# Layer 0 of a four-layer graph network: the one-hot edge types with edges along the columns, turned by TensorE before, loaded from memory after

## The chip, the cores and the metric

The kernel runs on one core of a Trainium2 chip. The metric is the device time of one execution in microseconds (us), the median of several runs. A core has five engines that run side by side, each through its own queue of instructions in order: TensorE (PE in the profile, its weight loads PEld), VectorE (DVE), ScalarE (ACT), GpSimd (POOL) and SyncE (SP), which here does nothing but start DMAs. An instruction may wait on semaphores that other engines or DMAs raise; while it waits, everything behind it in the same queue waits too. Sixteen DMA engines move data between memory (DRAM) and the on-chip buffer of 128 partitions (SBUF).

## What is computed

Four graph layers on 3125 nodes of 256 features and 50000 edges sorted by destination, each followed by a residual and a layer norm. The change touches layer 0 alone:

```python
e = edge_emb[edge_type]                       # 16 types
att_in = concat([x[src], x[dst], e, task])    # per edge, 4*256
edge_delta = tanh(gelu(att_in @ att_W1 + att_b1) @ att_W2 + att_b2)
edge_weight = 1.0 + edge_scale * edge_delta
messages = ((x[src] + e) @ msg_W + msg_b) * (1 + 0.5*tanh(gamma)) + beta
agg = segment_sum(messages * edge_weight, dst) / max(segment_sum(edge_weight, dst), 1)
# then an update MLP on [x, agg] and a layer norm
```

The kernel splits `att_in @ att_W1` into four products: the parts of the source and destination nodes are worked out once per node, the part of the type once per type (`ec`), and each edge adds three rows.

## The kernel before

**Tiling.** Edges are laid out by `bucket` into 416 slot tiles (`TT`) of 128 edges, one edge per partition; every slot tile belongs to one tile of 128 destination nodes (`tnode`). `s_src`, `s_dl` (place of the destination in its node tile) and `s_ty` (type) hold one column per slot tile. `segments` works out tables for the later layers, in four chunks of up to 128 slot tiles, with the slot tile on the partition and the edge along the columns; it writes `seg` and `rows` to DRAM.

**Layer 0's edge loop** (end of `layer0`) takes G = 4 slot tiles at a time, 104 groups, in a software pipeline: one turn of the loop issues `gathered` of group i, `attended` of group i-1 and `summed` of group i-2.

- `gathered(t0)`: four indirect DMAs on POOL (L509) fetch each edge's source row into `gb` (5 buffers; 640 floats a row: x and three bf16 thirds of its product, together the fp32 product). DVE builds the one-hot `oh[:, 0]` of destination places (L928), the one-hot of types (L931) in the first 16 columns of `gb`, and copies the latter three times side by side in bf16 into `oh[:, 1]` (L934, 48 of 128 columns; the rest was set to zero once, L918). TensorE transposes both (L939, eight 128x128 bf16 transposes into one PSUM tile `ohp`), and ACT copies the result to SBUF (L943, 128x1024), which gives `oht`: places, and types, with edges along the columns. Once every two groups SP stores the pair's places and turned places to `oh_d` and `oht_d` (L946), which layers 1 and 2 read.
- `attended`: per slot tile three products with `idb` add the source thirds (L956, two slot tiles at once), three products of the turned places with `xb` add the destination thirds (L961), and one product of the turned types with `ec` adds the type's part (L964; `ec` holds three bf16 thirds of the type product in rows 0 to 47). ACT applies GELU (L965), DVE multiplies by `att_W2` and sums (L967).
- `summed`: ACT takes tanh (L972), scales (L973) and weighs the places by the result (L976, `ohw`), TensorE sums the 128 edges of each slot tile by node (L979 into `pa`, three PSUM buffers), and DVE adds that to the accumulator (L981).

**What sets the order.** The Tile framework orders each engine's queue when the kernel is built, from dependencies and its own estimates, and inserts the semaphore waits; a buffer is written again only when all readers of the tile that held it are done. In the order built here PE runs, per turn: the transposes of group i+2, `attended` of group i+1 (L956, L961, L964 for two slot tiles, then again for two), the sums of group i (L979). DVE runs: two adds (L981) of group i-1 with the builds of types between them (L931, L934), the build of places (L928), two products L967, the first add of the next group, two more products L967, and so on. The fourth sum of a group needs the PSUM buffer that the first add of the same group frees, as `pa` has three.

Of the kernel before, what the change touches and what calls it, by code (L numbers as in the profile page):

```python
# [9 lines left out]
F32 = mybir.dt.float32  # L10
BF = mybir.dt.bfloat16
# [7 lines left out]
P = 128  # L19
# [14 lines left out]
class Net:  # L34
# [178 lines left out]
    def bucket(self, src, dst, type16, type8, weight, relations):  # L213
# [22 lines left out]
        self.seg = self.dram.tile([TT, 5, P], F32, name="seg")  # L236

        self.rows = self.dram.tile([NS, 2, S], F32, name="rows")
        self.astart, self.aend, self.anew = (c.tile([1, TT], F32, name=n) for n in ("astart", "aend", "anew"))
        self.tnode = c.tile([1, TT], I32, name="tnode")  # L240

        with tc.tile_pool(name="bk", bufs=1, side="right") as b:
# [40 lines left out]
            with tc.tile_pool(name="bkw", bufs=1, side="right") as w, tc.tile_pool(name="bkp", bufs=1, space=PSUM) as ps:  # L283
# [71 lines left out]
                nc.vector.tensor_single_scalar(bat, bat, D, op=ALU.mult)  # L355
                nc.scalar.dma_start(self.b_at, bat)

                self.segments(w, bd, nxt, prv, bdf, sel, kd)

    def segments(self, w, bd, nxt, prv, bdf, sel, kd):  # L360

        tc, nc, TT = self.tc, self.nc, self.TT
        C = bd.shape[1]
        flag = w.tile([P, 2, C, P], F32, name="flag")
        nc.vector.tensor_tensor(flag[:, 0], prv, bd, op=ALU.not_equal)
        nc.vector.tensor_tensor(flag[:, 1], nxt, bd, op=ALU.not_equal)
        zero = w.tile([P, P], F32, name="zero")
        nc.vector.memset(zero, 0.0)
        with tc.tile_pool(name="sgp", bufs=1, space=PSUM) as ps, tc.tile_pool(name="sg", bufs=2, side="right") as v:
            rows = ps.tile([1, 3, 512], F32, name="rows")  # L370
            for m0 in range(0, TT, P):
                M = min(P, TT - m0)
# [12 lines left out]
                nc.vector.tensor_scalar(low[:M], low[:M], float(P), None, op0=ALU.mult)  # L385
                sg = v.tile([P, 5, P], F32, name="sg")
                dl = v.tile([P, P], F32, name="dl")
                nc.vector.tensor_scalar(dl[:M], pk[:M, 0, :], low[:M], None, op0=ALU.subtract)
                ins = v.tile([P, P], F32, name="ins")
                nc.vector.tensor_scalar(ins[:M], dl[:M], 0.0, None, op0=ALU.is_ge)  # L390
                nc.vector.scalar_tensor_tensor(ins[:M], dl[:M], float(P), ins[:M], op0=ALU.is_lt, op1=ALU.mult)
                nc.vector.tensor_scalar(sg[:M, 0], ins[:M], -1.0, -NEG, op0=ALU.add, op1=ALU.mult)
                for n in (1, 2):
                    nc.vector.scalar_tensor_tensor(sg[:M, n], pk[:M, n, :], NEG, ins[:M],
                                                   op0=ALU.mult, op1=ALU.mult)
                nc.vector.tensor_tensor_scan(sg[:M, 3], zero[:M], sg[:M, 1], 0.0, op0=ALU.add, op1=ALU.min)
# [357 lines left out]
    def layer0(self, task, edge_emb, msg_W, msg_b, att_W1, att_b1, att_W2, att_b2, edge_scale,  # L754
# [9 lines left out]
        with ExitStack() as layer:  # L764
# [21 lines left out]
            ub2 = vec(up_b2, D, "ub2")  # L786
            lng = vec(ln_g, D, "lng")
            lnb = vec(ln_b, D, "lnb")
            ec = wp.tile([P, D], BF, name="ec")
            nc.vector.memset(ec, 0.0)  # L790
            one = wp.tile([P, 1], F32, name="one1")
            nc.vector.memset(one, 1.0)
            me = wp.tile([ET, D], F32, name="me")
# [2 lines left out]
            with tc.tile_pool(name="n0", bufs=2) as w, tc.tile_pool(name="m0", bufs=1) as wm, \  # L796
# [21 lines left out]
                E3 = 3 * ET  # L818
# [61 lines left out]
                nc.vector.tensor_scalar(fst[:, 2:3], self.pidx[:E3], float(2 * ET), None, op0=ALU.is_ge)  # L880
                nc.vector.tensor_add(fst[:, 1:2], fst[:, 0:1], fst[:, 2:3])
                nc.vector.tensor_scalar(fst[:, 1:2], fst[:, 1:2], -1.0, 1.0, op0=ALU.mult, op1=ALU.add)
                nc.vector.tensor_scalar(ecs, part[:, 0, :], fst[:, 0:1], None, op0=ALU.mult)
                for n, o in ((1, ecs), (2, ec[:E3])):
                    nc.vector.scalar_tensor_tensor(o, part[:, n, :], fst[:, n:n + 1], ecs,
# [25 lines left out]
            with tc.tile_pool(name="e0g", bufs=5) as gp, tc.tile_pool(name="e0", bufs=3) as w, \  # L911
# [1 line left out]

                places = [hp.tile([P, 2, 2, G, P], BF, name="places%d" % n) for n in range(2)]
                for n, oh in enumerate(places):
                    (nc.vector if n % 2 else nc.gpsimd).memset(oh[:, 1], 0.0)  # L918
                ohts = [None]

                def gathered(t0):
                    gb = gp.tile([P, G, ET + XA], F32, name="gb")
                    for j in range(G):
                        self.gather(gb[:, j, ET:], table, self.s_src, t0 + j)
                    g = t0 // G % 2
                    both = places[t0 // (2 * G) % len(places)]
                    oh = both[:, :, g]
                    nc.vector.tensor_tensor(  # L928
                        oh[:, 0], self.iota[:, None, :].to_broadcast([P, G, P]),
                        self.s_dl[:, t0:t0 + G][:, :, None].to_broadcast([P, G, P]), op=ALU.is_equal)  # L930
                    nc.vector.tensor_tensor(  # L931
                        gb[:, :, 0:ET], self.iota[:, None, :ET].to_broadcast([P, G, ET]),
                        self.s_ty[:, t0:t0 + G][:, :, None].to_broadcast([P, G, ET]), op=ALU.is_equal)
                    nc.vector.tensor_copy(oh[:, 1, :, 0:3 * ET].rearrange("p j (n e) -> p j n e", n=3),  # L934
                                          gb[:, :, None, 0:ET].to_broadcast([P, G, 3, ET]))
                    pt = ps.tile([P, 2, G, P], BF, name="ohp")
                    for n in range(2):
                        for j in range(G):
                            nc.tensor.transpose(pt[:, n, j, :], oh[:, n, j, :], self.idb)  # L939
                    if not g:  # L940
                        ohts[0] = hp.tile([P, 2, 2, G, P], BF, name="oht", bufs=2)
                    oht = ohts[0][:, :, g]
                    nc.scalar.copy(oht, pt)  # L943
                    if g:
                        for to, of in ((self.oh_d, both), (self.oht_d, ohts[0])):
                            nc.sync.dma_start(to[t0 // (2 * G)], of[:, 0].rearrange("p g j v -> p (g j v)"))  # L946
                    return t0, gb, oh, oht

                def attended(t0, gb, oh, oht):
                    hg = w.tile([P, G, D], F32, name="hg", bufs=2)  # L950
                    dl = w.tile([P, G], F32, name="dl")
                    for j0 in range(0, G, 2):
# [4 lines left out]
                        for j in (j0, j0 + 1):  # L957
                            q = pre[:, j - j0, :]
                            node = self.node_of(nc.tensor, t0 + j)
                            for n in range(3):  # L960
                                last = nc.tensor.matmul(q, oht[:, 0, j, :], xbr[:, ds(node * (3 * D) + n * D, D)],  # L961
                                                        start=False, stop=False)
                            self.used(nc.tensor, last)
                            nc.tensor.matmul(q, oht[:, 1, j, :], ec, start=False, stop=j > j0)  # L964
                        nc.scalar.activation(hg[:, j0:j0 + 2, :], pre, AF.Gelu)  # L965
                        for j in (j0, j0 + 1):
                            nc.vector.scalar_tensor_tensor(hg[:, j, :], hg[:, j, :], 1.0, aw2, op0=ALU.mult,  # L967
# [3 lines left out]
                def summed(t0, gb, oh, dl):  # L971
# [1 line left out]
                    nc.scalar.activation(dl, dl, AF.Identity, bias=one, scale=esc)  # L973
                    ohw = w.tile([P, G, P], F32, name="ohw", bufs=2)
                    for j in range(G):
                        nc.scalar.activation(ohw[:, j, :], oh[:, 0, j, :], AF.Copy, scale=dl[:, j:j + 1])  # L976
                    for j in range(G):
                        pa = ps.tile([P, SW], F32, name="pa", bufs=3)
                        nc.tensor.matmul(pa, ohw[:, j, :], gb[:, j, 0:ET + D], start=True, stop=True)  # L979
# [656 lines left out]
```

## Time and profile before

| | us |
|---|---|
| median of 3 runs (3344.36 to 3361.28) | 3351.46 |
| the profiled execution, whole | 3366.77 |
| its span, first to last instruction | 3365.0 |
| setup, sorting into slot tiles, node products of layer 0 | 0 to 215 |
| layer 0's edge loop | 215 to 800 |
| layer 0's node update, node products of layer 1 | 800 to 1170 |
| layer 1's edges, and its node update | 1170 to 1800 to 1970 |
| layer 2's edges, and its node update | 1970 to 2670 to 2830 |
| layer 3's edges and the output | 2830 to 3365 |

The stage bounds are read from the first and last starts of each stage's instructions. In the table of the span in 40 slices one slice is 84.1 us, so layer 0's edge loop is a little over half of the third slice up to the middle of the tenth. A group line of the profile gives line, engine, operation, output<-inputs, shape and count, then busy time and the mean of one, then the idle time before it and what ended most of that. A timeline line gives start, duration, engine, line, operation, count, and in brackets the idle time just before and what ended it.

### The profile page before, as it was taken

The numbers are of one execution on the slowest core, as the hardware profiler recorded it, in microseconds if no ns is written. First come the engines' busy times: TensorE is split into PE (matmuls) and PEld (weight loads), VectorE is DVE, ScalarE is ACT, GpSimd is POOL, SyncE is SP. The second block draws the span as 40 slices with busy tenths as digits, with TensorE's granted clock in tenths as the row PEclk, the third lists the DMA queues.
The fourth block names the chain that finished last, engine by engine and source line by source line (L and its number), as shares of the span: only waits on it lengthen the run. The fifth ranks groups of instructions, "written<-read, shape, count | busy, mean of one in ns | idle before, by whom it ended". The sixth has DMA issues, their size and how long they took to land. (4 is left out here: it accounts for less than half of the span.)

```text
span 3365.0 us, 50575 instructions
## 1 busy us (share of the span) xinstructions
PE 2690.9 (80%) x12679; PEld 1750.5 (52%) x12679; DVE 2267.3 (67%) x6030; ACT 1460.9 (43%) x4405; POOL 1832.7 (54%) x1850
## 2 busy tenths in 40 slices
PE   2779999999979767777775847888888886888885
PEld 1357777775546345555553525666666664333333
DVE  2546676667655479888886437888888873555555
ACT  1427777774456334545543215656656553000001
POOL 3037777771044166666661556766766202777773
PEclk9889999999989878888887968888888886656566
DMA  7249998894067877777774367877877235333333
GB/s 164 74 134 296 298 289 290 288 287 141 32 248 285 313 224 241 231 235 233 231 232 132 123 209 200 227 226 223 228 223 225 78 125 221 106 106 105 105 106 92
DMA packets 240632, 658.40 MB, mean 196 GB/s; under 512 B 47976, under 2 KB 87028, under 8 KB 234029
## 3 DMA queue, kind: packets, MB, share of 16 engines
q0 software_dynamic: 132400, 484.37, 46.9%
q1 hardware_dynamic: 104278, 167.53, 15.2%
q10 hardware_dynamic: 3676, 3.23, 0.5%
q8 instruction: 122, 2.00, 0.2%
q14 instruction: 156, 1.28, 0.1%
HBM read 513.06 MB, written 151.58 MB: 198 GB/s over the span
## 5 line engine op out<-in xcount | busy, mean ns | idle before, releaser
L509 POOL DMA_INDIRECT gb<-table,s_src x832 | 859.1, 1033 | 371.6 <-issue 201.2
L706 PE MATMUL pr<-r,oh 128*128 128x260 f32 x2496 | 735.8, 441 | 82.2 <-DVE acc L711 32.6
L706 PEld LDWEIGHTS pr<-r,oh 128*128 128x128 f32 x2496 | 503.2, 217 | 219.5 <-issue 37.2
L1509 POOL DMA_INDIRECT ring<-table,b_rel x391 | 369.7, 946 | 317.9 <-DVE oh L1519 199.1
L701 ACT ACTIVATE r<-gb,ex 128x64 f32<-128x64 f32 x2080 | 522.3, 335 | 0.0
L509 POOL DMA_INDIRECT gb<-table,s_rel x416 | 404.4, 972 | 205.8 <-issue 110.0
L711 DVE TENSOR_TENSOR acc<-acc,pr 128x260 f32 (+1 forms) x832 | 457.9, 550 | 73.0 <-PE pr L706 59.4
L1538 PE MATMUL pa<-ring,oh 128*128 x832 | 420.5, 617 | 92.3 <-DMA ring<-table,b_rel 44.6
L1538 PEld LDWEIGHTS pa<-ring,oh 128*128 128x128 f32 x832 | 190.7, 278 | 322.4 <-DVE oh L1519 210.8
L1545 DVE TENSOR_TENSOR x<-x,pa 128x256 f32 x416 | 175.2, 421 | 227.8 <-PE pa L1538 225.6
L1237 PE MATMUL pqe<-q_all,oht 128*128 x1248 | 207.1, 304 | 94.6 <-DVE pd L1242 78.7
L693 ACT CAST oh<-ohb 128x512 f32<-128x512 bf16 x208 | 128.3, 618 | 314.2 <-PE pr L706 284.3
L589 ACT ACTIVATE r<-mv,eps 128x4 f32<-128x4 f32 (+2 forms) x31 | 9.1, 295 | 527.8 <-DVE mv L575 524.4
L697 DVE TENSOR_TENSOR r<-gb,ex 128x512 f32<-128x512 f32 (+1 forms) x208 | 225.7, 1086 | 13.3 <-ACT ex L666 9.0
L979 PE MATMUL pa<-gb,ohw 128*128 128x272 f32 x832 | 223.4, 402 | 4.5 <-DVE acc L981 2.9
L1237 PEld LDWEIGHTS <-oht 128*128 128x128 bf16 x1248 | 130.6, 106 | 128.4 <-issue 87.6
L961 PE MATMUL pre<-xb,oht 128*128 x1248 | 193.7, 273 | 0.0
L981 DVE TENSOR_TENSOR acc<-acc,pa 128x272 f32 x416 | 179.7, 432 | 5.1 <-PE pa L979 2.8
L928 DVE TENSOR_TENSOR places<-iota,s_dl 128x512 bf16<-128x512 f32 x104 | 71.9, 691 | 160.8 <-ACT ohw L976 160.8
L956 PE MATMUL pre<-gb,idb 128*128 128x512 bf16 x624 | 169.3, 380 | 5.3 <-DMA gb<-table,s_src 5.3
L967 DVE SCALAR_TENSOR_TENSOR hg<-hg,aw 128x256 f32<-128x256 f32 x416 | 159.3, 420 | 16.4 <-ACT hg L965 16.4
L979 PEld LDWEIGHTS pa<-gb,ohw 128*128 128x128 f32 x832 | 141.2, 190 | 54.6 <-issue 34.0
(383 smaller groups left out, 4302.0 us busy)
## 6 DMA issues: line engine op xcount, KB each, us to landing
ohb<-oh_d SPq DMA_DIRECT2D x104, 256.0 KB
oht<-oht_d SPq DMA_DIRECT2D x104, 256.0 KB
table<-row SPq DMA_DIRECT2D x25, 1024.0 KB
gb<-table,s_src POOLq DMA_INDIRECT x832, 4.5
oh_d<-places SPq DMA_DIRECT2D x52, 256.0 KB
oht_d<-oht SPq DMA_DIRECT2D x52, 256.0 KB
sgm<-seg SPq DMA_DIRECT2D x26, 320.0 KB
gb<-table,s_rel POOLq DMA_INDIRECT x416, 4.7
```

What stands on the lines that cost most here:

```text
L509: self.nc.gpsimd.indirect_dma_start(out=out, out_offset=None, in_=table, in_offset=bass.IndirectOffsetOnAxis(ap=idx[:, t:t + 1], axis=0))
L697: nc.vector.tensor_mul(r[:, :, :nd, :hw], v[:, :, :nd, :], ex[:, :nd, s0:s0 + G].rearrange("p h t -> p t h")[:, :, :, None].to_broadcast([ ...
L701: nc.scalar.activation(r[:, j, h, :hw], v[:, j, h, :], AF.Copy, scale=ex[:, h, s0 + j:s0 + j + 1])
L706: nc.tensor.matmul(pr[:, n, :HB * F], oh[:, j, :], r[:, j, n * HB:(n + 1) * HB, :].rearrange("p h f -> p (h f)"), start=True, stop=True)
L711: self.used(nc.vector, nc.vector.tensor_add(a, a, pr[:, :, :HB * F]))
L961: last = nc.tensor.matmul(q, oht[:, 0, j, :], xbr[:, ds(node * (3 * D) + n * D, D)], start=False, stop=False)
L979: nc.tensor.matmul(pa, ohw[:, j, :], gb[:, j, 0:ET + D], start=True, stop=True)
L981: self.used(nc.vector, nc.vector.tensor_add(a, a, pa))
L1237: last = nc.tensor.matmul(pq[:, j, :], oht[:, j, :], q_all[:, ds(node * (3 * D) + n * D, D)], start=n == 0, stop=n == 2)
L1509: st = nc.gpsimd.indirect_dma_start(out=ring[:, at:at + D], out_offset=None, in_=table, in_offset=bass.IndirectOffsetOnAxis(ap=b_rel[:, b: ...
L1538: last = nc.tensor.matmul(pa, oh[:, j, :], ring[:, ds(at, D)], start=True, stop=True)
L1545: self.used(nc.vector, nc.vector.tensor_add(a, a, pa))
```

## The change

The types with edges along the columns no longer come from `gathered`.

- `segments` multiplies the selection of each chunk with the types too (four more fp32 products into the PSUM tile `pk`, behind the reading of its last column), ACT copies the result to bf16, and SP stores it in a new DRAM tensor `ty_d`: one row of 128 types per slot tile.
- For every pair of groups (8 slot tiles) `spread` loads the 1024 types, 2 KB, into all 128 partitions: one DMA of 128 rows of 2 KB that all come from the same 2 KB of DRAM, 256 KB written. The tile `types` has three buffers. The load for pair k+1 is asked for at the start of pair k.
- `attended` begins with a DVE comparison in place (128x512 bf16): each partition's own type number, `own` (0 to 15 three times, -1 from partition 48 on), against the loaded types. This is the one-hot that the product with `ec` takes.
- Four of the eight transposes, the DVE copy (L934) and half of ACT's copy (L943) go, as does the clearing of the old tiles on DVE and POOL.
- `places` and `oht` are now tiles of a pair of groups, two buffers each, taken anew for every pair, where `places` were two fixed tiles before.

```diff
-                places = [hp.tile([P, 2, 2, G, P], BF, name="places%d" % n) for n in range(2)]
-                for n, oh in enumerate(places):
-                    (nc.vector if n % 2 else nc.gpsimd).memset(oh[:, 1], 0.0)
-                ohts = [None]
+                both, types_of = [None], [None]
+
+                def spread(t0):
+                    types_of[0] = t = hp.tile([P, 2, G, P], BF, name="types", bufs=3)
+                    nc.sync.dma_start(t.rearrange("p g j e -> p (g j e)"), bass.AP(
+                        tensor=self.ty_d.tensor, offset=self.ty_d.offset + t0 * P, ap=[[0, P], [1, 2 * G * P]]))
+
+                spread(0)
...
                     g = t0 // G % 2
-                    both = places[t0 // (2 * G) % len(places)]
-                    oh = both[:, :, g]
+                    if not g:
+                        both[0] = [hp.tile([p, 2, G, P], BF, name=n, bufs=2) for p, n in (
+                            (P, "places"), (P, "oht"))] + [types_of[0]]
+                        if t0 + 2 * G < TT:
+                            spread(t0 + 2 * G)
+                    oh, oht, ty = (b[:, g] for b in both[0])
...
-                    nc.vector.tensor_copy(oh[:, 1, :, 0:3 * ET].rearrange("p j (n e) -> p j n e", n=3),
-                                          gb[:, :, None, 0:ET].to_broadcast([P, G, 3, ET]))
-                    pt = ps.tile([P, 2, G, P], BF, name="ohp")
-                    for n in range(2):
-                        for j in range(G):
-                            nc.tensor.transpose(pt[:, n, j, :], oh[:, n, j, :], self.idb)
-                    if not g:
-                        ohts[0] = hp.tile([P, 2, 2, G, P], BF, name="oht", bufs=2)
-                    oht = ohts[0][:, :, g]
+                    pt = ps.tile([P, G, P], BF, name="ohp")
+                    for j in range(G):
+                        nc.tensor.transpose(pt[:, j, :], oh[:, j, :], self.idb)
                     nc.scalar.copy(oht, pt)
...
+                def attended(t0, gb, oh, oht, ty):
+                    nc.vector.tensor_scalar(ty, ty, own, None, op0=ALU.is_equal)
...
-                            nc.tensor.matmul(q, oht[:, 1, j, :], ec, start=False, stop=j > j0)
+                            nc.tensor.matmul(q, ty[:, j, :], ec, start=False, stop=j > j0)
...
+                for k in range(C):
+                    nc.tensor.matmul(pk[:M, 3, :], sel[:, k, m0:m0 + M], f16[:, k, :], start=k == 0, stop=k == C - 1)
+                ty = v.tile([P, P], BF, name="ty")
+                nc.scalar.copy(ty[:M], pk[:M, 3, :])
+                nc.sync.dma_start(self.ty_d[m0:m0 + M], ty[:M])
```

More of the change, by code (lines that the diff above doesn't have):

```diff
@@ L238, in bucket @@
         self.rows = self.dram.tile([NS, 2, S], F32, name="rows")
+        self.ty_d = self.dram.tile([TT, P], BF, name="ty_d")
         self.astart, self.aend, self.anew = (c.tile([1, TT], F32, name=n) for n in ("astart", "aend", "anew"))
@@ L356, in bucket, with segments @@
                 nc.scalar.dma_start(self.b_at, bat)
-                self.segments(w, bd, nxt, prv, bdf, sel, kd)
-    def segments(self, w, bd, nxt, prv, bdf, sel, kd):
+                self.segments(w, bd, nxt, prv, bdf, sel, kd, f16)
+    def segments(self, w, bd, nxt, prv, bdf, sel, kd, f16):
         tc, nc, TT = self.tc, self.nc, self.TT
@@ L788, in layer0 @@
             lnb = vec(ln_b, D, "lnb")
+            E3 = 3 * ET
             ec = wp.tile([P, D], BF, name="ec")
             nc.vector.memset(ec, 0.0)
+            own = wp.tile([P, 1], F32, name="own")
+            nc.vector.memset(own, -1.0)
             one = wp.tile([P, 1], F32, name="one1")
@@ L817, in layer0 @@
                 ul = film_loads(ua_W1, ua_b1, ua_W2, ua_b2, "ua")
-                E3 = 3 * ET
                 emb = wm.tile([E3, D], F32, name="emb")
@@ L882, in layer0 @@
                 nc.vector.tensor_scalar(fst[:, 1:2], fst[:, 1:2], -1.0, 1.0, op0=ALU.mult, op1=ALU.add)
+                nc.vector.scalar_tensor_tensor(own[:E3], fst[:, 2:3], 2.0, fst[:, 1:2], op0=ALU.mult, op1=ALU.add)
+                nc.vector.scalar_tensor_tensor(own[:E3], own[:E3], -float(ET), self.pidx[:E3], op0=ALU.mult, op1=ALU.add)
                 nc.vector.tensor_scalar(ecs, part[:, 0, :], fst[:, 0:1], None, op0=ALU.mult)
@@ L925, in gathered @@
                     g = t0 // G % 2
-                    both = places[t0 // (2 * G) % len(places)]
-                    oh = both[:, :, g]
+                    if not g:
[4 more added lines that the diff above has]
+                    oh, oht, ty = (b[:, g] for b in both[0])
                     nc.vector.tensor_tensor(
-                        oh[:, 0], self.iota[:, None, :].to_broadcast([P, G, P]),
+                        oh, self.iota[:, None, :].to_broadcast([P, G, P]),
                         self.s_dl[:, t0:t0 + G][:, :, None].to_broadcast([P, G, P]), op=ALU.is_equal)
@@ L933, in gathered @@
                         self.s_ty[:, t0:t0 + G][:, :, None].to_broadcast([P, G, ET]), op=ALU.is_equal)
-                    nc.vector.tensor_copy(oh[:, 1, :, 0:3 * ET].rearrange("p j (n e) -> p j n e", n=3),
-                                          gb[:, :, None, 0:ET].to_broadcast([P, G, 3, ET]))
-                    pt = ps.tile([P, 2, G, P], BF, name="ohp")
-                    for n in range(2):
-                        for j in range(G):
-                            nc.tensor.transpose(pt[:, n, j, :], oh[:, n, j, :], self.idb)
-                    if not g:
-                        ohts[0] = hp.tile([P, 2, 2, G, P], BF, name="oht", bufs=2)
-                    oht = ohts[0][:, :, g]
+                    pt = ps.tile([P, G, P], BF, name="ohp")
+                    for j in range(G):
+                        nc.tensor.transpose(pt[:, j, :], oh[:, j, :], self.idb)
                     nc.scalar.copy(oht, pt)
                     if g:
[L945 to L949, printed above, removed]
+                        for to, of in zip((self.oh_d, self.oht_d), both[0]):
+                            nc.sync.dma_start(to[t0 // (2 * G)], of.rearrange("p g j v -> p (g j v)"))
+                    return t0, gb, oh, oht, ty
+                def attended(t0, gb, oh, oht, ty):
+                    nc.vector.tensor_scalar(ty, ty, own, None, op0=ALU.is_equal)
                     hg = w.tile([P, G, D], F32, name="hg", bufs=2)
@@ L960, in attended @@
                             for n in range(3):
-                                last = nc.tensor.matmul(q, oht[:, 0, j, :], xbr[:, ds(node * (3 * D) + n * D, D)],
+                                last = nc.tensor.matmul(q, oht[:, j, :], xbr[:, ds(node * (3 * D) + n * D, D)],
                                                         start=False, stop=False)
                             self.used(nc.tensor, last)
-                            nc.tensor.matmul(q, oht[:, 1, j, :], ec, start=False, stop=j > j0)
+                            nc.tensor.matmul(q, ty[:, j, :], ec, start=False, stop=j > j0)
                         nc.scalar.activation(hg[:, j0:j0 + 2, :], pre, AF.Gelu)
@@ L975, in summed @@
                     for j in range(G):
-                        nc.scalar.activation(ohw[:, j, :], oh[:, 0, j, :], AF.Copy, scale=dl[:, j:j + 1])
+                        nc.scalar.activation(ohw[:, j, :], oh[:, j, :], AF.Copy, scale=dl[:, j:j + 1])
                     for j in range(G):
```

## The prediction

> **What bounds the kernel now.** Only layer 0's edge loop changes in weight, so I read it first in the 40 slices and by stage, then its waits, then one turn of the loop.
>
> ```profile
> PE   2779999999979767777775847888888886888885
> PEclk9889999999989878888887968888888886656566
> DMA  7249998894067877777774367877877235333333
> ```
>
> ```profile
> 215.00:800.00 585.00, 572.78 (x3952) 412.82 (x3952) 402.58 (x1572) 410.82 (x936) 415.06 (x417) 0.99 0.87 281
> 800.00:1170.00 370.00, 322.01 (x1485) 185.40 (x1485) 214.08 (x483) 170.17 (x309) 82.84 (x85) 0.94 0.55 207
> ```
>
> By stage (PE, PEld, DVE, ACT, POOL busy, granted clock, DMA share, GB/s) PE is busy 573 of 585 us in the loop, at clock 0.99; the DMA engines 87%, DVE and ACT about 70%. So PE sets the pace, and DMA is close behind. The waits from 300 to 760 show what stands just behind PE:
>
> ```profile
> DVE places L928 <- ACT ohw L976: 134.9, 83, 1.7
> PEld pa L979 <- issue: 27.6, 84, 0.7
> ```
>
> Both come once a group: DVE waits 1.6 us for the last `ohw` before it may build places again, and PE has a hole of 0.3 us inside the sums. One turn on the timeline ties them together:
>
> ```profile
> 502.17 0.69 DVE L928 TENSOR_TENSOR places<-iota,s_dl 128x512 bf16<-128x512 f32 x1 [1.66 <-ACT ohw L976]
> 502.78 0.42 DVE L967 SCALAR_TENSOR_TENSOR hg<-hg,aw 128x256 f32<-128x256 f32 x1
> 502.85 0.60 ACT L965 ACTIVATE hg<-pre 128x512 f32<-128x512 f32 x1 [0.23 <-PE pre L964]
> ...
> 503.51 0.44 DVE L981 TENSOR_TENSOR acc<-acc,pa 128x272 f32 x1
> ...
> 504.06 0.30 PEld L979 LDWEIGHTS pa<-gb,ohw 128*128 128x128 f32 x2 [0.30 <-issue]
> ...
> 504.63 0.61 PE L939 MATMUL ohp<-idb,places 128*128 128x128 bf16 x8
> ...
> 505.07 0.81 PE L956 MATMUL pre<-gb,idb 128*128 128x512 bf16 x3
> ...
> 506.62 0.98 ACT L976 ACTIVATE ohw<-places,dl 128x128 f32<-128x128 bf16 x3
> ...
> 507.64 0.69 DVE L928 TENSOR_TENSOR places<-iota,s_dl 128x512 bf16<-128x512 f32 x1 [1.65 <-ACT ohw L976]
> ...
> 508.31 0.60 ACT L965 ACTIVATE hg<-pre 128x512 f32<-128x512 f32 x1 [0.23 <-PE pre L964]
> ```
>
> The reader is to see a chain without slack: places (502.17), two products, the first add (503.51, done 503.95), which frees the third PSUM buffer back for the fourth sum (its weights at 504.06), the transposes, `attended`, and its last GELU at 508.31. Whatever is put on DVE between the places and that first add, PE pays for. The stores give the pair's length:
>
> ```profile
> L946 SPq DMA_DIRECT2D oh_d<-places x42: 319/320/320, 305.1 to 755.4; - x42
> ```
>
> 41 pairs in 450.3 us: 10.98 us a pair of groups.
>
> **What goes.** PE: eight transposes take 504.63 to 505.07, so four are 0.22 us a group, 104 x 0.22 = 23 us in the loop: the whole gain if PE stays the bound. DVE's L934 (279 ns) and about 0.37 us of ACT's copy (992 ns against 618 ns of the 128x512 copy L693) lie beside PE's work: nothing by themselves. POOL's clearing (0.95 us at 215.14) stood before the first gather, on which PE's start waits: 1 us gained.
>
> **What comes in setup.** Four times four fp32 products (16 instructions of this kind took 1.95 us at 184.47, so about 1 us a chunk), a copy and a 32 KB store. In a chunk PE waits over 2 us for DVE's segment work (2.08 us at 189.35), and the products fall into that hole; ACT is idle. If the cover failed: 4 x (1.0 + 0.4, the 392 ns of a 128x128 ACT operation, L976) = 6 us. I take 0. The store and the first load end before the first gather lands (224.2).
>
> **What comes in the loop.** Per pair one DMA of 256 KB on SP (0.32 us of issue; SP is nearly idle), and two comparisons on DVE. A comparison of 128x512 is not in the trace; the nearest rows are the comparison with constants of 128x128 in 227 ns, and the scaling by a column, 128x512 fp32, in 473 ns (L1258). It works on bf16: I take 0.30, bounds 0.20 and 0.47.
>
> More than these durations, the order built for the changed kernel decides. For pair 30/31:
> - SP starts the load of types 30/31 when PE has done the last `ec` product of group 25: three buffers, and that one held types 24/25.
> - DVE's comparison for group 30, which waits for that load, stands between the third and fourth add of group 24, six groups ahead of its use. Behind it on DVE: that fourth add, the places of 28 **and** 29 back to back (both wait for the last `ohw` of 25, since the pair's tile is taken as one), two products of 26, the comparison for 31, the first add of 25.
> - On PE the fourth sum of group 25 waits for that add, then come the transposes, `attended` of 27, and its last `ec` product, which releases the next load.
>
> So one loop closes per pair, with the load's landing in it. "Eight slot tiles ahead" counts to the use; DVE asks for the types about 2.5 us after the load may start (group 24's sums follow group 25's `ec` at once, and the adds follow the sums).
>
> Its length, from the timeline above (start to start): the last `ec` to SP 0.05; the landing L; comparison 0.30 and fourth add 0.35; places to the end of the first add 503.95 - 502.17 = 1.78, plus a second build of places 0.61 (502.17 to 502.78) and a comparison 0.30: 2.69; the end of that add to the next last GELU 508.31 - 503.95 = 4.36, less 0.22 of transposes: 4.14. Sum: L + 7.53. Against 10.98: **L - 3.45 us a pair**, once for each of 49 loads (the first three find free buffers).
>
> L, from issue to landing of 256 KB, is not in the trace for this stage. Rows around it: 320 KB gathers here, and 256 KB loads of one-hots, seen where layer 2's chain of waits holds them:
>
> ```profile
> DMA to landing us min/median/max: 4.2/5.4/6.5
> ```
>
> ```profile
> 1993.69 14.90 DMA oht<-oht_d
> 2015.84 5.21 DMA oht<-oht_d
> ```
>
> A gather's issue takes 0.95 us against 0.32, and 64 KB less at 281 GB/s is 0.2 us: 5.4 - 0.6 - 0.2 = 4.6. Bounds: 4.2 - 0.8 = 3.4, and 6.5. L = 4.6 gives 1.15 us a pair, 49 x 1.15 = 56 us. Ends: at 3.4 nothing; at 6.5, with comparisons of 0.47, 49 x (3.05 + 0.34) = 166 us.
>
> **A rule against this.** The Trainium skill, "DMA: Bandwidth & Descriptors", section "Anatomy of one DMA", prices a DMA at about 2.0 us fixed plus its bytes at 436 GB/s; by that estimate 256 KB land in 2.6 us, before DVE asks, and the loop would be held by the places alone (below, +3 us). The gathers here never landed in under 4.2 us, in a stage whose engines are 87% busy, so I go by the row.
>
> **Sum.** 56 - 1 = +55 us. The profiled execution (3366.77, span 3365.0, 1.8 around it) lies 15 us above the median; the difference is added to the median: 3351.5 + 55 = **3406 us**.
>
> **Rivals.**
> - *Faster:* PE stays the bound. It needs the types at DVE in time (L under about 3.4) and the doubled places to fit: 3351 - 23 - 1 = 3327. For it: DVE is only 69% busy. Against it: 4.2 us as the shortest landing, and the chain without slack.
> - *No change:* the load is in time, but places 28 and 29 in a row hold PE. The last `ohw` ended 507.60, 4.75 us after GELU's 502.85; a shorter copy (0.37) and products not behind places in odd groups (0.17) make it 4.21. 4.21 + 2.69 + 4.14 = 11.04 a pair: +3 us, 3354. Gain given back, and the point from which L decides is 3.5.
> - *DMA becomes the bound:* a group moves 281 x 5.49 = 1.54 MB and would move 1.67; at 87% busy the engines have room for 281/0.87 = 323 GB/s, so 5.2 us a group, just under the 5.27 that PE would need. It could only take the gain away, 3354 or so, and counts with the one above.
> - *Much slower:* 128 reads of the same 2 KB crowd, or PE's holes of 2 us a pair lower its clock. No row shows the first in this stage; L at 6.5 gives 3351 + 166 = 3517. For the second, 800 to 1170 us shows clock 0.94 with PE 87% busy, which is what PE would be here (10.5 of 12.1 us): 6% of the 4.14 us in the loop, 12 us more.
>
> The Trainium skill, "TensorE: Matmul & The Clock Gate", Part 1, lets the clock fall only after an idle window of about 3.4 us; holes of 2 us would then cost nothing.
>
> **How the numbers follow.** Load-bound as summed, 0.63; no change 0.17; PE-bound and faster 0.08; much slower 0.12. 0.5% of the time, 17 us, is about what this measurement can tell. Slower is 0.63 + 0.12 = 0.75. The range leaves out the faster case (0.08) and most of the last: 3350 to 3480, the upper end being L = 6.0 (125 us); the likeliest case alone spans 3370 to 3480.
>
> **What would show it.** Right: the loop from 215 to about 855, pairs of 12.1 us; DVE's longest wait in it is the comparison for a DMA, about 2 us once a pair; PE's sums wait for DVE's add, some 1.5 us a pair; PE under 90% there; later stages as before. Wrong: stores 10.5 us apart (PE-bound), a wait on `ohw` and none on the DMA (places), or landings far from 4.6 us.

## The result, and the profile after

The changed kernel takes 3446.03 us (median of 4 runs, 3441.2 to 3449.32) against 3356.19 us for the kernel before (4 runs, 3344.36 to 3361.28; the three of the table above and one more): a ratio of 1.0259, 95% interval 1.0238 to 1.028. It is slower, as forecast, by 90 us where 55 were forecast. The profiled execution took 3445.55 us with a span of 3443.6: 78.6 us more span than before. (The spans differ by less than the medians because the profiled execution of the kernel before, 3366.77 us, lay 10.6 us above the median of its four runs.)

The 40 slices of the changed kernel:

```profile
PE   2878888888879968777776675888888787888885
PEclk9889999999989978888888787898888995555566
DMA  7248888888226877777775447787878425333333
```

PE showed mostly 9 in the loop of layer 0; now it shows 8, for longer. The stage view (columns as for the kernel before):

```profile
215.00:880.00 665.00, 567.02 (x3530) 395.58 (x3528) 416.29 (x1561) 355.66 (x931) 400.77 (x416) 0.96 0.82 268
880.00:1250.00 370.00, 323.70 (x1495) 185.62 (x1495) 219.23 (x498) 172.22 (x315) 82.82 (x85) 0.95 0.54 204
```

The loop's stage is 80 us longer and PE is busy in 85% of it, not 98%. The stage behind it is as before, 370 us with PE busy 324 (322 before). The waits of the loop from 300 to 760 us (engine, line, who was waited for; us in all, times, longest):

```profile
ACT dl L988 <- DVE hg L983: 154.3, 73, 4.4
DVE types L965 <- DMA types<-ty_d: 91.7, 36, 3.7
...
PEld pa L995 <- issue: 74.2, 37, 2.2
...
PE pa L995 <- DVE acc L997: 63.2, 49, 1.8
...
SPq L933 <- PE pre L980: 195.5, 37, 6.7
```

The second line is new: once a pair DVE stands 2.5 us at the comparison, waiting for the load. The last line is SP's queue: each load waits there for PE's last `ec` product of an earlier group before it is issued. One turn of the timeline shows both ends of the loop:

```profile
505.71 0.32 SPq L933 DMA_DIRECT2D types<-ty_d  x1
505.71 0.60 ACT L981 ACTIVATE hg<-pre 128x512 f32<-128x512 f32 x1 [0.57 <-PE pre L980]
...
511.24 0.35 DVE L965 TENSOR_SCALAR types<-types,own 128x512 bf16<-128x512 bf16 x1 [3.10 <-DMA types<-ty_d]
511.51 0.43 DVE L997 TENSOR_TENSOR acc<-acc,pa 128x272 f32 x1
511.86 1.29 DVE L949 TENSOR_TENSOR places<-iota,s_dl 128x512 bf16<-128x512 f32 x2
513.06 0.42 DVE L983 SCALAR_TENSOR_TENSOR hg<-hg,aw 128x256 f32<-128x256 f32 x1
...
513.75 0.35 DVE L965 TENSOR_SCALAR types<-types,own 128x512 bf16<-128x512 bf16 x1
514.01 0.43 DVE L997 TENSOR_TENSOR acc<-acc,pa 128x272 f32 x1
...
514.60 0.70 PE L995 MATMUL pa<-gb,ohw 128*128 128x272 f32 x2 [1.81 <-DVE acc L997]
...
518.59 0.32 SPq L933 DMA_DIRECT2D types<-ty_d  x1
```

From the issue to the comparison 5.53 us pass, from there to the next issue 7.35. Between 300 and 760 us the two medians are 5.05 and 7.34 us, the two means 4.98 and 7.60. The issues themselves give the pair (durations, then first and last start):

```profile
L933 SPq DMA_DIRECT2D types<-ty_d x37: 319/320/320, 303.4 to 756.5; - x37
```

36 pairs in 453.1 us are 12.59 us each, against 10.98: 1.61 x 49 = 79 us, which is the whole of the span's 78.6. That the second mean lies above its median comes from five of the 36 turns, in which this part took 9.0 to 9.2 us. In one of them, between 321 and 332 us, three stretches show the granted clock (third figure from the end):

```profile
321.00:325.40 4.40, 2.20 (x12) 1.21 (x11) 4.23 (x16) 0.64 (x2) 1.11 (x2) 1.00 0.96 359
325.40:328.80 3.40, 3.40 (x14) 1.82 (x12) 0.93 (x4) 2.46 (x7) 2.70 (x3) 0.50 0.52 145
328.80:332.00 3.20, 3.20 (x22) 2.46 (x21) 2.12 (x10) 0.95 (x3) 1.15 (x2) 1.00 0.84 247
```

After the turn's holes PE ran 3.4 us at half clock, and its rows are longer there, here and then in a turn without that:

```profile
327.07 0.42 PE L980 MATMUL pre<-ec,types 128*128 128x256 bf16 x1
...
516.33 0.27 PE L980 MATMUL pre<-ec,types 128*128 128x256 bf16 x1
```

Five such stretches of 3.4 us lie between 300 and 760 us (at 325, 476, 674, 701 and 738), one in each of the five longer turns. At about 1.7 us each they make 0.23 us a pair.

What is left of the span nearly cancels: the loop's first add starts 4.7 us later (238.5 against 233.8), and all that follows its last add takes 6.8 us less (2558.7 against 2565.5).

### The profile page after: what moved, and what is told of

Same layout as the page of the kernel before. It is cut to its first block, busy times and chain, and to the rows that moved or that the text cites. A ratio compares the mean times of both kernels' runs of the same rounds, so it can differ in the third digit from the quotient of the medians.

```text
span 3443.6 us, 49933 instructions
## 1 busy us (share of the span) xinstructions
PE 2703.0 (78%) x12295; PEld 1744.7 (51%) x12295; DVE 2284.3 (66%) x6032; ACT 1408.8 (41%) x4409; POOL 1816.5 (53%) x1849
## 5 line engine op out<-in xcount | busy, mean ns | idle before, releaser
L516 POOL DMA_INDIRECT gb<-table,s_src x832 | 843.4, 1014 | 604.7 <-issue 199.2
L1554 PE MATMUL pa<-ring,oh 128*128 x832 | 431.2, 631 | 81.3 <-DMA ring<-table,b_rel 41.1
L977 PE MATMUL pre<-xb,oht 128*128 x1248 | 200.6, 280 | 0.0
L1253 PEld LDWEIGHTS <-oht 128*128 128x128 bf16 x1248 | 131.1, 107 | 123.9 <-issue 83.1
L972 PE MATMUL pre<-gb,idb 128*128 128x512 bf16 x624 | 177.2, 394 | 6.6 <-DMA gb<-table,s_src 6.6
L977 PEld LDWEIGHTS <-oht 128*128 128x128 bf16 x1248 | 125.6, 101 | 64.5 <-issue 6.8
```

Source lines behind the costliest of these rows:

```text
L516: self.nc.gpsimd.indirect_dma_start(out=out, out_offset=None, in_=table, in_offset=bass.IndirectOffsetOnAxis(ap=idx[:, t:t + 1], axis=0))
L972: nc.tensor.matmul(pre, self.idb, xa[:, :, n * D:(n + 1) * D], start=n == 0, stop=False)
L977: last = nc.tensor.matmul(q, oht[:, j, :], xbr[:, ds(node * (3 * D) + n * D, D)], start=False, stop=False)
L1253: last = nc.tensor.matmul(pq[:, j, :], oht[:, j, :], q_all[:, ds(node * (3 * D) + n * D, D)], start=n == 0, stop=n == 2)
L1554: last = nc.tensor.matmul(pa, oh[:, j, :], ring[:, ds(at, D)], start=True, stop=True)
```

## The experiments

**Theory:** the landing of the load sits in the pair's loop because VectorE's comparison, early on its in-order queue, stands ahead of adds that PE waits for. **Rivals:** (1) the extra transfers cost the time; (2) building places two at a time does; (3) the prefetch is too shallow; (4) reading one 2 KB row 128 times makes the load slow.

The first four kernels ran on one chip, beside 17 runs of the kernel before (3363.68 us).

**late.** The kernel's list `uses` holds VectorE's adds in order; the comparison is held back behind the fifth last of them.

```diff
-                    nc.vector.tensor_scalar(ty, ty, own, None, op0=ALU.is_equal)
+                    with tc.issue_after(self.uses[nc.vector.engine][-5]) if len(self.uses.get(nc.vector.engine, [])) > 4 else ExitStack():
+                        nc.vector.tensor_scalar(ty, ty, own, None, op0=ALU.is_equal)
```

> One edit to the changed kernel: on VectorE's queue the comparison of a group's types stands five recorded operations later, behind the third or fourth add of the group before its own (comparison 26 behind the add 23.75) instead of ahead of the adds of group 23; the loads, their three buffers and the double build of places stay. The load for 26 is then issued after the last ec product of group 21, a whole pair loop before the comparison wants it. THEORY (the landing time of the load sits in the pair loop only because the comparison stands early on VectorE's queue): VectorE's wait for the load falls from 2.5 us a pair (91.7 us in 36) to under 0.2, the pair from 12.59 us to between 10.54 (PE bound) and 11.04 (places back to back), so the time to between 3330 and 3365 us. RIVAL 1 (the transfers themselves cost the time, by crowding the DMA engines): still 3430 to 3450. RIVAL 2 (the two builds of places in a row are the larger part): 3395 to 3420.

Measured: 3349.35 us, ratio 0.9956 (0.9941 to 0.9972). The load's issues and the waits of this kernel, 300 to 760 us:

```profile
L933 SPq DMA_DIRECT2D types<-ty_d x43: 319/320/320, 302.8 to 743.9; - x43
```

```profile
ACT dl L989 <- DVE hg L984: 104.7, 87, 1.4
POOL gb L516 <- issue: 98.1, 322, 0.3
DVE hg L984 <- ACT hg L982: 58.9, 44, 1.4
ACT hg L982 <- PE pre L981: 52.8, 88, 0.6
DVE places L949 <- ACT ohw L993: 37.7, 44, 0.9
PEld pa L996 <- issue: 19.8, 43, 0.5
```

42 pairs in 441.1 us: 10.50 us each. Not one wait for the load is left, though the same 256 KB are moved, the tile has the same three buffers, and places are still built in twos. The place of one instruction on VectorE's queue is worth 2.09 us a pair. That takes down rivals 1, 2 and 3 as the cause of the loss. The kernel beats the one before by 0.4%, which is small, but the interval leaves out 1: its loop is 25 us shorter (540.9 us from first to last add, 565.8 before), but it begins 7 us later. The view of 300 to 760 us shows how full it is:

```profile
300.00:760.00 460.00, 457.37 (x2983) 330.03 (x2982) 350.31 (x1312) 299.64 (x791) 353.31 (x351) 1.00 0.96 326
```

PE is busy 457 of 460 us, and the DMA engines 96%, at 326 GB/s.

**place.** The comparison stays early; places go back to two fixed tiles.

```diff
+                fixed = [hp.tile([P, 2, G, P], BF, name="places%d" % n) for n in range(2)]
...
-                        both[0] = [hp.tile([p, 2, G, P], BF, name=n, bufs=2) for p, n in (
-                            (P, "places"), (P, "oht"))] + [types_of[0]]
+                        both[0] = [fixed[t0 // (2 * G) % 2], hp.tile([P, 2, G, P], BF, name="oht", bufs=2), types_of[0]]
```

> One edit to the changed kernel: places lies in two fixed tiles, as in the kernel before, so that VectorE builds the places of one group at a time (0.65 us) instead of two in a row (1.29 us); the load and the early comparison stay. THEORY: the wait for the load stays in the pair loop; only one build of places instead of two lies between the comparison and the adds that the PE waits for, so the pair falls by at most 0.65 us, from 12.59 to 11.94, and the time to between 3414 and 3446 us, with 1.5 to 3 us of wait for the load a pair left. RIVAL 2 (the double build is what slows the loop): 3365 or less, the wait for the load down to little.

Measured: 3413.69 us, ratio 1.015 (1.0125 to 1.0176). Its wait for the load:

```profile
DVE types L965 <- DMA types<-ty_d: 98.8, 39, 4.0
```

Still 2.5 us a pair. From issue to comparison 5.17 us, from there to the next issue 6.75, by 0.6 less than 7.34: one build of places (0.61 us) less between comparison and add, and nothing else. The second part of the sum is what the prediction made it. Its issues lie 11.79 us apart, a little under the 11.94 expected, and the time is 0.3 us below its range: the shorter holes of this kernel (up to 1.4 us on PE, 1.8 in the changed kernel) were followed by one stretch at half clock between 300 and 760 us, not five.

**b6.**

```diff
-                    types_of[0] = t = hp.tile([P, 2, G, P], BF, name="types", bufs=3)
+                    types_of[0] = t = hp.tile([P, 2, G, P], BF, name="types", bufs=6)
```

> One edit to the changed kernel: the tile types has six buffers instead of three, so each load may be issued six slot tiles of groups earlier than now. In the built order the comparison moves as far ahead as the load does: comparison 28 stands before the places of group 20 (with three buffers: 26), and the load for 28 still waits for the last ec product of group 17 (with three buffers: 23). THEORY: the same loop between load, comparison and product remains, 12.4 to 12.8 us a pair, and the time stays at 3430 to 3450 us (at most the three last pairs no longer wait). RIVAL 3 (the prefetch is too shallow: three buffers are too few for a load of 5 us): no wait for the load, 3330 to 3365 us.

Measured: 3438.15 us, ratio 1.0233 (1.0201 to 1.0264).

```profile
DVE types L965 <- DMA types<-ty_d: 88.8, 38, 3.5
```

4.8 us from issue to comparison, 7.35 after it, and 12.29 us a pair (12.4 to 12.8 expected): the same loop. Twice the buffers bring next to nothing, because in the built order the comparison moves forward with the load. A deeper prefetch helps only if what consumes it stays where it was.

**noload.** No loads in the loop, and the comparison writes a tile of its own.

```diff
-                        if t0 + 2 * G < TT:
-                            spread(t0 + 2 * G)
...
-                    nc.vector.tensor_scalar(ty, ty, own, None, op0=ALU.is_equal)
+                    out = hp.tile([P, G, P], BF, name="typed", bufs=6)
+                    nc.vector.tensor_scalar(out, ty, own, None, op0=ALU.is_equal)
+                    ty = out
```

> The changed kernel without the loads inside the loop: one tile of types is loaded once, ahead of it, and each comparison reads that tile and writes one of six buffers of its own, so that the types of all but the first pair are wrong; no comparison waits for a DMA. Places are still built two at a time. THEORY: the loop falls to its floor without the load, between 10.54 us a pair (PE bound) and 11.04 (places back to back), so 3330 to 3360 us. RIVAL 2 (the double build of places costs most of the 90 us): 3395 to 3430 us.

Measured: 3368.37 us, ratio 1.0009 (0.9995 to 1.0022), 8 us above the range given, which was set from the 3351 to 3356 us of the kernel before elsewhere (here 3364). The stores of this kernel:

```profile
L959 SPq DMA_DIRECT2D oh_d<-places x42: 319/320/320, 304.5 to 754.5; - x42
```

41 pairs in 450.0 us: 10.98 us, at the upper end of the expectation for the pair; the loop starts 10 us later than before (first add 244.2). So the pair can be taken apart: 10.50 us is PE's own (late); 0.48 more is the early order on VectorE (noload: comparison and two builds of places ahead of the adds); 1.61 more comes with the load (12.59), 0.23 of it by PE's half clock after the holes, of which late and noload have none between 300 and 760 us. With the comparison late, the double build costs nothing on this chip: it waits 0.9 us a pair, and PE is busy all the same.

The next seven runs came to two other chips, on which the kernel before takes 3975.98 and 3974.22 us. Only ratios can be compared there, and what stands in the last section limits them.

**rows** and **rows_2** (one kernel, two chips). Each partition reads 2 KB of its own:

```diff
-                        tensor=self.ty_d.tensor, offset=self.ty_d.offset + t0 * P, ap=[[0, P], [1, 2 * G * P]]))
+                        tensor=self.ty_d.tensor, offset=self.ty_d.offset, ap=[[3 * P, P], [1, 2 * G * P]]))
```

> The changed kernel with one edit to the load: partition p reads 2 KB from 768 p bytes on, so that the 128 partitions read 128 different places instead of all the same 2 KB; 256 KB as before, the same queue, the same waits, other types (so the attention is that of other types). THEORY (the load takes some 5 us whatever it reads; only its place in the pair loop matters): landing 4.5 to 5.5 us, pair 12.3 to 12.9 us, 3430 to 3455 us. RIVAL 4 (128 reads of the same 2 KB get in each other's way, and make the landing 5.0 us instead of the 4.1 us of the loads of the same size in layer 1): landing 4.1 us, pair 11.7 us, 3395 to 3410 us.

> The same kernel as in the run rows: each partition reads 2 KB of its own, 768 bytes further on than the partition before it, instead of all reading the same 2 KB; other types, the same amount. THEORY (a load of 256 KB takes some 5 us in this loop whatever it reads): 4.8 to 5.3 us from issue to comparison, 12.2 to 12.7 us a pair, 1.020 to 1.030 of the kernel before. RIVAL 4 (reads of the same 2 KB get in each other's way): 4.1 us as for the loads of layer 1, or less, 11.5 us a pair, 1.012 or below.

Measured: 3937.55 us, ratio 0.9879 (0.9808 to 0.9949), and 3946.12 us, ratio 0.9932 (0.9895 to 0.997).

**part** and **part_2.** The expectations speak of 84 partitions and 168 KB; that was a slip: with 16 types in three parts there are 48, so a load is 96 KB.

```diff
-                    nc.sync.dma_start(t.rearrange("p g j e -> p (g j e)"), bass.AP(
+                    nc.sync.dma_start(t[:E3].rearrange("p g j e -> p (g j e)"), bass.AP(
...
-                    nc.vector.tensor_scalar(ty, ty, own, None, op0=ALU.is_equal)
+                    nc.vector.tensor_scalar(ty[:E3], ty[:E3], own[:E3], None, op0=ALU.is_equal)
...
-                            nc.tensor.matmul(q, ty[:, j, :], ec, start=False, stop=j > j0)
+                            nc.tensor.matmul(q, ty[:E3, j, :], ec[:E3], start=False, stop=j > j0)
```

(The access pattern's count of partitions becomes `E3` as well.)

> The changed kernel with the load, the comparison and the product cut to the 84 partitions that hold a type's rows of ec (the other 44 rows of ec are zero): 168 KB a load instead of 256 KB. THEORY: the pair is the landing of the load plus 7.4 us, so it falls by what the landing falls; by bytes alone 5.0 us would fall to 3.3, with a fixed part of 2 us or more it falls to 4.0 to 4.6. That gives 11.4 to 12.2 us a pair and 3390 to 3430 us. RIVAL (the landing is a queueing time that does not depend on the load's size): 3436 to 3450 us. Comparison and products keep their 0.35 us and 0.27 us.

> The same kernel as in the run part: load, comparison and product cut to 84 of the 128 partitions, 168 KB a load. In the three kernels that keep the early comparison, the pair was the time from a load's issue to its comparison (5.05, 5.18 and 4.81 us) plus 6.75 or 7.35 us. THEORY: the same sum holds here with 7.35 us and a shorter landing; with the bytes alone in proportion 5.05 would become 3.3, with a fixed part of 2 us 4.0: 10.7 to 11.5 us a pair, 3350 to 3395 us, 0.998 to 1.011 of the kernel before. RIVAL 5 (the landing is time in the queue behind the gathers, whatever the load's size): 5 us, 12.4 us a pair, 1.022 to 1.028.

Measured: 3926.33 us, ratio 0.9861 (0.9826 to 0.9896), and 3923.23 us, ratio 0.9899 (0.9848 to 0.9951). On these chips from issue to comparison pass 3.3 and 3.2 us (rows and rows_2, medians) and 3.2 and 3.5 us (part and part_2), and from there to the next issue about 10 (9.8 to 10.7), where 7.35 was expected. All four expectations miss: the wait for the load is a smaller part of the turn there (1.1 us a pair in rows, 2.5 in the changed kernel). The load is also quicker, with the DMA engines nearly as busy (share 0.80 in rows, 0.83 in the changed kernel); why, the runs don't show.

**before_load.** The kernel before with one load more a pair, into a tile that nothing reads.

```diff
+                        t = hp.tile([P, 2, G, P], BF, name="types", bufs=3)
+                        nc.sync.dma_start(t.rearrange("p g j e -> p (g j e)").bitcast(F32), bass.AP(
+                            tensor=self.x_in.tensor, offset=self.x_in.offset + t0 // (2 * G) % 12 * 512, ap=[[0, P], [1, 512]]))
```

> The kernel before with one load more in each pair: SyncE reads the same 2 KB of the input x into all 128 partitions of a tile that nothing reads (256 KB, the traffic of the changed kernel). Nothing on VectorE or PE waits for it. THEORY (the transfers cost nothing unless something waits for them): 3350 to 3365 us, 10.9 to 11.1 us a pair. RIVAL 1 (traffic): gathers and stores land later, and the time goes to 3390 us or more.

Measured: 3974.07 us, ratio 1.003 (0.9986 to 1.0074). This experiment failed in its design: with nobody to wait for, all 52 loads were issued between 217 and 319 us, so the traffic lay at the head of the loop, not in each pair. late is the better evidence on traffic.

**late_place** and **late_place_2**: the edits of late and place together.

> The two edits of the runs before together: the comparison five operations later on VectorE's queue, and places in two fixed tiles built one group at a time. VectorE's order is then that of the kernel before, with a comparison of 0.35 us in place of the copy of the types, and PE has four transposes fewer a group. THEORY: neither the load nor the double build is waited for, and the loop goes to the PE's bound, 10.54 us a pair with four transposes of 0.055 us less a group: 3325 to 3345 us, faster than the kernel before. RIVAL 1 (traffic): 3390 us or more. RIVAL (VectorE and ScalarE set the pace once the transposes are gone): 3350 to 3360 us, no gain.

> The same kernel as in the run late_place, on another chip if there is one that runs the kernel before in its usual 3360 us: the comparison five operations later on VectorE's queue, and places built one group at a time. The comparison alone moved gave 10.50 us a pair, which is PE's own work (10.54 expected). THEORY: PE is the bound already, so the second edit adds nothing: 10.4 to 10.5 us a pair and 0.993 to 0.998 of the kernel before. RIVAL 2 (the double build costs something still): 10.3 us a pair or less, 0.990 or below.

Measured: 3872.86 us, ratio 0.9766 (0.9707 to 0.9824), and 3898.1 us, ratio 0.9813 (0.9757 to 0.987). Faster than before by about 2%, the best of the kernels on these chips (12.5 and 12.7 us a pair from first to last add, 14.7 in before_load). The second ratio lies below the 0.993 to 0.998 of its theory, in the range of its rival; but that range was set for the other sort of chip. Whether the second edit adds anything to the first stays open: late did not run here, and this kernel not where late did.

**three.** One kernel with three kinds of load in turn, so that the landing is compared inside one loop (again 48 partitions and 96 KB where the expectation says 84 and 168). It ran on a chip where the kernel before takes 3363.52 us.

```diff
+                    kind = t0 // (2 * G) % 3
+                    n = E3 if kind == 2 else P
+                    nc.sync.dma_start(t[:n].rearrange("p g j e -> p (g j e)"), bass.AP(
+                        tensor=self.ty_d.tensor, offset=self.ty_d.offset + (0 if kind == 1 else t0 * P),
+                        ap=[[3 * P if kind == 1 else 0, n], [1, 2 * G * P]]))
```

> The changed kernel with its three buffers of types loaded in three ways, in turn, so that one run compares them in the same loop: A as in the changed kernel (all 128 partitions read the same 2 KB), B 128 partitions that each read 2 KB from 768 bytes further on (other types in these pairs), C the same 2 KB into 84 partitions only (168 KB). Comparison and product take 84 partitions in all pairs. What is read is the median landing of each kind and, where VectorE waits for it, the time from issue to comparison. THEORY (the landing is mostly time behind the gathers and stores on busy DMA engines, so address pattern and a third of the bytes change little): A, B within 0.3 us of each other, 4.8 to 5.2 us on a chip that runs the kernel before in 3360 us, 3.0 to 3.6 us on one that runs it in 3975; C 0.3 to 0.8 us less than A. RIVAL 4 (reads of the same 2 KB get in each other's way): B 0.5 us or more below A. RIVAL (bytes alone): C a third below A, 3.3 us against 5.0. A pair stays its own issue-to-comparison time plus 7.35 us on the first sort of chip; there the time is 1.015 to 1.026 of the kernel before, on the other sort 0.985 to 0.995.

Measured: 3469.87 us, ratio 1.0301 (1.0267 to 1.0334). Medians over the loop, from issue to comparison:

| load | us | then to the next issue |
|---|---|---|
| A: 128 partitions, the same 2 KB | 5.21 | 8.07 |
| B: 128 partitions, each its own 2 KB | 5.01 | 8.07 |
| C: 48 partitions, the same 2 KB | 3.84 | 8.23 |

B is 0.2 us under A, so rival 4 falls: reading one row 128 times costs at most some 4% of the time to the comparison. C lands 1.37 us earlier with 160 KB less, outside the range expected of it for a third less, but the load was cut by more than that; in a line through both points, an estimate, 3.0 us would be left for no bytes at all. The second column and the time missed: they should have been 7.35 and at most 1.026. The waits show why:

```profile
PEld L983 <- issue: 60.2, 286, 0.2
```

PE's weight loads stand 0.21 us ahead of each of the 286 48-row products; 8 a pair, of which four lie between a comparison and the next issue. That would be 0.8 us, an estimate, and 0.72 more was measured there. It is a cost of the cut, not of the load.

## Why the prediction came out as it did

- **The bound and the loop: right.** The order read out of the built kernel (SP's load behind the `ec` product of five groups earlier, the comparison between two adds, both builds of places, then the add that PE wants) is what the timeline shows, and late and place confirm it by taking out one link each. The sign, the wait and the path were foreseen; the size was put too low, 55 us against 79 in the span and 90 in the medians.
- **L + 7.53 us: the 7.53 right, but for PE's clock.** 7.34 measured in the median, and 7.37 in the mean of the turns without half clock: 0.16 x 49 = 8 us less.
- **L = 4.6 us: this term was too small.** 4.98 us in the mean of 36 pairs (5.05 in the median): 0.38 x 49 = 19 us more. It was inside the bounds (3.4 to 6.5), and the time inside the range. The weak step is "5.4 - 0.6 - 0.2": the 5.4 stands for the 42 of 338 gathers whose landing the trace has, and a gather turned out a rough measure of a load. In place, gathers land in 5.2 us in the median (39 of 312 on record), and from the load's issue to its comparison pass 5.2; in three, gathers land in 4.1 us (36 of 287) and the same load still takes 5.2. Why a load of 256 KB takes these 5 us isn't taken apart.
- **PE's clock after the holes: left out of the sum.** It stood among the rivals, at 12 us. Measured: 0.23 us a pair, 49 x 0.23 = 11 us, from 3.4 us at half clock in about one turn of seven. No hole was longer than 2.2 us in the row of PE's weight loads or 1.8 us in that of its products, so the prediction's last word on it, that holes of 2 us would cost nothing, isn't what the trace shows. Between 300 and 760 us b6, with the same holes, has three such stretches, place with shorter ones one, late and noload, whose holes on PE stay under 0.5 us, none. Why some turns and not others, stays open; so does three, which has none, with holes of over 1 us in five places only.
- **The sum again:** 56 + 19 - 8 + 11 = 78 us, against 79 measured for the loop (1.61 x 49).
- **The rule weighed there** (the Trainium skill, "DMA: Bandwidth & Descriptors", "Anatomy of one DMA — SWDGE (gpsimd) path": 2.0 us fixed and the bytes at 436 GB/s, by which 256 KB are an estimate of 2.6 us) is half of what the loop shows, 5.05 us at a DMA share of 0.83 between 300 and 760 us. The page gives this fit for DMAs that GpSimd issues; this load is issued by SyncE. Going by the row was right.
- **Faster (3327): wrong for this order, right as PE's floor.** 10.54 us a pair was foreseen, 10.50 came in late.
- **No change (11.04 a pair): the floor was real** (10.98 without the load), and lay under the load-bound loop as the prediction had it.
- **DMA as the bound: not reached.** Room was put at 323 GB/s; late moves 326 at a share of 0.96 and still keeps PE full.
- **Setup, taken as 0: wrong, and its bound of 6 us too low.** The stores of the segment rows, one a chunk, show it, before and then after:

```profile
L403 SPq DMA_DIRECT2D seg<-sg x4: 317/320/343, 190.0 to 211.1; - x4
```

```profile
L410 SPq DMA_DIRECT2D seg<-sg x4: 313/320/320, 187.0 to 214.9; - x4
```

  Three chunks took 21.1 us and now take 27.9: 2.3 us each, 6.8 in all (27.9 to 30.5 us in the other five kernels of this setup on such chips). Less a start that was 3 us earlier, that is most of the 4.7 us. The products did not fall into the hole. In each chunk VectorE now stands 1.3 to 1.4 us until ACT has copied the types out of `pk`, ahead of the segment work that the hole waits for; what makes the rest isn't separated:

```profile
184.69 0.35 DVE L395 TENSOR_SCALAR dl<-pk,low 128x128 f32<-128x128 f32 x1 [1.26 <-ACT ty L391]
```

## What to carry to other kernels

A load ahead of time is only as early as the first instruction that waits for it stands on its in-order queue: look in the built order for what is queued behind that wait, and who needs it, before counting buffers. If the consumer moves forward with every buffer that is added, more buffers change nothing; hold the consumer back behind work that must be done first, which here turned 2.6% slower into 0.4% faster. Price a load that may enter a loop by a load of its own kind under such traffic; the estimate from gathers of the same stage came out 0.4 us too low here. A size's worth is to be read from two sizes in one loop, as in three. And where a change opens holes in PE's work, put the clock after them into the sum, not only among the rivals.

## What the runs showed of the hardware that was not expected

- **Chips differ far more than the runs on one.** Two chips gave 3976 and 3974 us for the kernel before, 18% over the 3356 to 3364 of the others; the mean granted clock of the kernels run there was 0.803 to 0.820, against 0.838 to 0.847 elsewhere, which is far less of a difference. On these chips engines wait for PE's results longer than PE's rows say. In before_load, 300 to 700 us:

```profile
ACT hg L968 <- PE pa L982: 117.4, 48, 2.7
PEld pa L982 <- ACT hg L968: 108.2, 49, 4.8
```

  The GELU, which needs the `ec` product, starts only when sums that stand behind that product already run. From the recorded end of the `ec` product to the GELU the median is 0.65 us in late_place there, and 0.04 us in the changed kernel. The ends of matmuls are modelled (the Trainium skill, "Perfetto Trace Analysis", "Tensor Engine Instruction (MATMUL, LD_WEIGHTS)", says that the profiler estimates them), so PE may be slower there than its rows show; why, stays open. What may follow for the change: where PE holds the loop more strongly, four transposes less weigh more and the wait for the load less (28 us in 25 pairs in rows against 92 in 36). rows, which is the changed kernel but for addresses, was faster than before by about 1% on both. The changed kernel itself was not run there, so that its sign turns is argued, not shown.
- **A product with 48 of 128 rows costs PE more than the full one.** Its weight load takes 93 ns against 100 and its product 280 ns against 277 (means of three and of the changed kernel), but PE's weight loads stand 0.21 us ahead of each, where ahead of the 294 full ones they stood 3.9 us in all. The load of 48 rows starts 4 ns before its own product, in the median, the full one 107 ns; from the start of the product ahead to the start of the product behind 0.42 us pass, against 0.22. The Trainium skill, "TensorE: Matmul & The Clock Gate", "Step-by-step: what each phase is for", lets PE pull a weight load ahead of running matmuls when the row groups don't conflict or the load goes to the background buffer; whichever of these it was, loads of 48 rows between loads of 128 were not pulled ahead here.
